# Queries of two attention layers: projected per pair of head groups, unpadded, and spread by transfers

## The chip, the cores and the metric

The kernel runs on one core of one Trainium2 chip. The core has five engines that work side by side: TensorE (matmuls, in the profile PE, its weight loads PEld), VectorE (DVE), ScalarE (ACT), GpSimd (POOL) and SyncE (SP, which issues transfers). Each engine has a queue of its own and takes its instructions in order. The metric is the device time of one execution in microseconds; the whole program, four layers, is one launch.

## What is computed

The reference is a stack of four layers, each a cross attention followed by a feed-forward part with experts. The change touches the cross attentions of layers 2 and 3. Their core, cut to what matters:

```python
# layer 2: B=2 batches, T=512 queries, T_ctx=1024 keys, 16 heads of 16
q = (x @ Wq + bq).reshape(B, T, H, D).transpose(0, 2, 1, 3)
kv = context @ Wkv + bkv
k, v = jnp.split(kv, 2, axis=-1)
att = jnp.einsum('bhtd,bhsd->bhts', q, k) * (1.0 / jnp.sqrt(D))
att = jnp.where(causal[None, None], att, -jnp.inf)
att = jax.nn.softmax(att, axis=-1)
y = jnp.einsum('bhts,bhsd->bhtd', att, v)
return y.transpose(0, 2, 1, 3).reshape(B, T, C) @ Wp + bp

# layer 3: no causal mask, no bias, and rotary embedding of queries and keys
def _apply_rope(t):
    cos, sin = _rope_tables(t.shape[2], t.shape[3], t.dtype)
    return t * cos[None, None] + _rotate_half(t) * sin[None, None]
q = _apply_rope((x @ Wq).reshape(B, Nq, H, hd).transpose(0, 2, 1, 3))
k = _apply_rope(k)
attn = jax.nn.softmax(jnp.einsum('bhqd,bhkd->bhqk', q, k) * scale, axis=-1)
```

Here `x` is the layer-normed state, 2 x 512 rows of 256 numbers. All is done in 32-bit floats.

## The kernel before, in words

`attend16` is the attention of layers 2 and 3. A head has only 16 dimensions, while the matmul array has 128 rows. So four heads make a group, and each head gets 32 rows of the array: 16 for its dimensions, one for its key maximum (row 16) and the rest zero. There are 2 batches x 4 groups = 8 groups, numbered 0 to 7; groups 0 to 3 are batch 0. The tile `qT` holds the queries of one group in this padded form, 128 rows by 512 queries; `kT` holds its keys the same way.

The padding is made by the weights: `Wq_pad` (`_pad_cols`, L2095) has zero columns where a head's 16 rows end, so one projection of a group gives `qT` padded. That is `prep(n)` (L1541): two matmul calls over the two halves of the 256 input channels (`mm2`, L187 to L190), 128 output rows by 512 queries. A float32 matmul call shows in the trace as two matmul records. In layer 2 the bias is added by VectorE as the sum is read (L1548). In layer 3, except for group 0, ScalarE copies the sum (L1559), one more matmul with a permutation matrix turns it (L1562, tile `rot`), VectorE multiplies that by the sines (L1564, `rs`), and GpSimd multiplies the copy by the cosines and adds (L1565, L1566).

The work of a group is cut into slots, 8 in layer 2 and 16 in layer 3. In slot h of group n, TensorE computes two score blocks of a first pass over group n (L1624, queries against keys), of which VectorE takes the maxima (L1628 with the mask in layer 2, L1633 in layer 3), and two score blocks of a second pass over an earlier group (L1683), whose exponentials ScalarE writes as `p` (L1684). The second pass runs LAG = slots + 2 behind the first. `with_maxima` (L1640) lies between them: it turns the negated maxima into row 16 and adds them to `qT`, which gives `qA`, the queries of the second pass. `product` (L1649) multiplies `p` with the values, and after the last one ScalarE copies the sum (`ou`, L1664). Its reciprocals take a way through memory: `Inverse` (L216) packs the rows by four transfers (L225), VectorE inverts them (L228, kept in program order on its engine), and five more transfers (L230, L233) spread them over a tile with the tag `rec`, of which there are two buffers. `divide` (L1693) multiplies on GpSimd.

All score, projection and rotation results go to banks of PSUM taken from one ring of seven (`bank`, L1529). A bank is taken again when its reader is done.

The order on TensorE is the program's order (`pe_in_order`, L1751). Extra work is cut into pieces that are called between slots (`Pieces`, L262): `prep` of the next group is put in front of the list at h = 0 of each group (L1756), and one piece is called in a slot, in odd slots of layer 3 and even ones of layer 2 (not in slot 0). Keys of the next group are fetched at h = 2 by SP (`fetch16`, L1476: four transfers of 16 rows for `kT`, L1480, and in layer 3 eight more for the turned keys, L214) and rotated at h = 8 (`rotate`, L200, on VectorE and GpSimd). The expert weights of layer 2's feed-forward part (L661, four transfers of 2 MB) are held back until group 0's maxima are in, and then run during the first groups. The parameters of an attention (`params16`, L1432) are loaded by SP during the feed-forward part before it.

Before the change no transfer of `attend16` is issued by ScalarE; elsewhere in the kernel ScalarE issues stores of keys and values (L806, L825).

Of the kernel before, what the change touches and what calls it, by code (L numbers as in the profile page):

```python
# [10 lines left out]
F32 = mybir.dt.float32  # L11
I32 = mybir.dt.int32
AF = mybir.ActivationFunctionType
# [4 lines left out]
P = 128  # L18
D = 256
B = 2  # L20
N = 512
S = 1024
# [11 lines left out]
def tile_kernel(ctx: ExitStack, tc: tile.TileContext, d: dict, out: bass.AP):  # L34
    nc = tc.nc
# [164 lines left out]
    def rotate(k, turned, cos, sin, pin=keep):  # L200


        for hf in range(2):
            hs = slice(hf * 512, (hf + 1) * 512)
            pin(nc.vector.tensor_mul(turned[:, hs], turned[:, hs], sin[:, hs]))  # L205
            pin(nc.gpsimd.tensor_mul(k[:, hs], k[:, hs], cos[:, hs]))  # L206
            nc.gpsimd.tensor_add(k[:, hs], k[:, hs], turned[:, hs])  # L207
# [947 lines left out]
    pre = ExitStack()  # L1155
# [276 lines left out]
    def params16(L, rotary, bias):  # L1432

        pre = ExitStack()
        cp = pre.enter_context(tc.tile_pool(name=f"{L}p", bufs=1, reuse_waits="tile"))
        bq = bvp = perm16 = wqr = cos = sin = None
        loads = []

        def ld(pool, shape, src, name):
            t = pool.tile(shape, F32, tag=name, name=name)  # L1440
            loads.append((t, src))
            return t

        def ld_rows(pool, src, name):
            rows, cols = src.shape
            return ld(pool, [P, rows // P, cols], src.rearrange("(t p) f -> p t f", p=P), name)

        def ld_bc(pool, src, name):
            return ld(pool, [P, src.shape[0]], src.partition_broadcast(P), name)

        one17 = ld(cp, [P, 1], d["c_one17"], "one17")
        if bias:
            bq, bvp = ld(cp, [P, 4], d[f"{L}_bq_pad"], "bq"), ld(cp, [P, 4], d[f"{L}_bv_pad"], "bvp")
        if rotary:
            cos, sin = ld(cp, [P, S], d["c_cos16"], "cos"), ld(cp, [P, S], d["c_sin16"], "sin")
            perm16 = ld(cp, [P, P], d["c_perm16"], "perm16")
            wqr = ld_rows(cp, d[f"{L}_Wq_turned"], "wqr")
        wq = ld_rows(cp, d[f"{L}_Wq_pad"], "wq")
        wo = ld_rows(cp, d[f"{L}_Wo_pad"], "wo")
        bo = ld_bc(cp, d[f"{L}_bo"], "bo")  # L1460
        sel16 = ld(cp, [P, P], d["c_sel16"], "sel16")
        cmask = None
        if not rotary:
            cmask = cp.tile([P, 4, P], F32, tag="cmask", name="cmask")
            nc.gpsimd.memset(cmask[:, 0:3, :], 0.0)
            make_causal_mask(nc, cmask[:, 3, :], NEG)
            cmask = cmask.rearrange("p t f -> p (t f)")

        return pre, cp, loads, (perm16, one17, wqr, bvp, bq, cos, sin, wq, wo, bo, sel16, cmask)

    def key_rows(k, one17, engine):

# [29 lines left out]
    def attend16(L, params, nkt, causal, rotary, front, norm, V, keys):  # L1502
# [11 lines left out]
        with (  # L1514
# [2 lines left out]
            tc.tile_pool(name=f"{L}t", bufs=2, reuse_waits="tile") as tmp,  # L1517
            psum(1, f"{L}ps") as ps,
        ):
            perm16, one17, wqr, bvp, bq, cos, sin, wq, wo, bo, sel16, cmask = params  # L1520
            kTs, turns, nms, fetched_keys = keys
            if nms is None:
                nms = maxima16(cp)
# [8 lines left out]
            groups = [(b, g) for b in range(B) for g in range(4)]  # L1532
            G = [dict() for _ in groups]
            oTs, ready = {}, []

            def fetch(n):
                G[n].update(kT=kTs[n % 3], v=V[groups[n][0]])
                if n >= fetched_keys:
                    fetch16(L, n, kTs[n % 3], turns[n % 2] if rotary else None, keep if n > 1 else as_is)

            def prep(n):  # L1541

                b, g = groups[n]
                qT = G[n]["qT"] = kp.tile([P, N], F32, tag="qT", name="qT")
                pq = bank("pq")
                mm2(pq, wq, slice(g * P, (g + 1) * P), xT, slice(b * N, (b + 1) * N))
                if not rotary:
                    nc.vector.tensor_scalar(qT, pq, bq[:, g : g + 1], None, ALU.add)  # L1548
                    yield
                    return  # L1550
                if n == 0:
                    rot = bank("rot")
                    mm2(rot, wqr, slice(0, P), xT, slice(0, N))
                    nc.vector.tensor_mul(qT, pq, cos[:, 0:N])
                    rs = tmp.tile([P, N], F32, tag="rs", name="rs")
                    nc.vector.tensor_mul(rs, rot, sin[:, 0:N])
                    nc.vector.tensor_add(qT, qT, rs)
                    return
                nc.scalar.copy(qT, pq)  # L1559
                yield  # L1560
                rot = bank("rot")
                nc.tensor.matmul(rot, perm16, qT, start=True, stop=True)  # L1562
                rs = tmp.tile([P, N], F32, tag="rs", name="rs")
                nc.vector.tensor_mul(rs, rot, sin[:, 0:N])  # L1564
                nc.gpsimd.tensor_mul(qT, qT, cos[:, 0:N])  # L1565
                nc.gpsimd.tensor_add(qT, qT, rs)  # L1566
                yield
# [171 lines left out]

            fetch(0)  # L1740
            fetch(1)
            norm_to(xn, X, norm)
            for _ in into_xT(0):
                pass
# [6 lines left out]
            with pe_in_order():  # L1751
                while t <= NG * slots + LAG + 6 or pieces.queue:
                    n, h = divmod(t, slots)
                    steps = range(t, t + (2 if n >= NG or n == 0 else 1))
                    if h == 0 and n + 1 < NG:
                        pieces.add(prep(n + 1), 2 if rotary else 1, True)  # L1756
                    if h == 2 and 0 < n < NG - 1:
                        fetch(n + 1)
                    if t == 2:
# [3 lines left out]
                        pieces.add(second_batch(), 7)  # L1763
                    if rotary and h == 8 and 0 < n < NG - 1:
                        rotate(G[n + 1]["kT"], turns[(n + 1) % 2], cos, sin)
                    for first in ((False, True) if h % 2 == 0 else (True, False)):
                        if first and n < NG:
                            first_pass(n, h)
                        elif not first:
                            for u in steps:  # L1770
                                m, k = divmod(u - LAG, slots)
                                if 0 <= m < NG:
                                    second_pass(m, k)
# [317 lines left out]
def _per_partition(v):  # L2091
    return v.reshape(2, P).T


def _pad_cols(w):  # L2095

    p = np.zeros((w.shape[0], 16, 32), w.dtype)
    p[:, :, :16] = w.reshape(-1, 16, 16)
    return p.reshape(w.shape[0], 512)


def _arrays(i):
# [20 lines left out]
        "L3_onw_p": _per_partition(i["L3_ffn_out_norm_w"]),  # L2123
        "L2_bo": i["L2_xattn_bp"],
        "L3_bo": i["L3_xattn_bo"],
        "L2_bq_pad": _pad_cols(i["L2_xattn_bq"][None]).reshape(4, P).T,
        "L2_bk": _per_partition(i["L2_xattn_bkv"][:D]),
        "L2_bv_pad": _pad_cols(i["L2_xattn_bkv"][None, D:]).reshape(4, P).T,
        "c_sign": np.tile(np.repeat(np.float32([-1.0, 1.0]), 32), 2)[:, None],
# [18 lines left out]
    a["c_cos64"], a["c_sin64"] = _rotary_table(S, 64, 64)  # L2148
    a["c_cos16"], a["c_sin16"] = _rotary_table(S, 16, 32)

    a["c_cos16"].reshape(4, 32, S)[:, 16] = 1.0
    for n in (
        "L0_xattn_Wq", "L0_xattn_Wkv", "L0_xattn_Wo", "L0_xattn_bo",
# [4 lines left out]
    ):  # L2158
        a[n] = i[n]
    for L, wo in (("L2", "L2_xattn_Wp"), ("L3", "L3_xattn_Wo")):  # L2160
        a[f"{L}_Wq_pad"] = _pad_cols(i[f"{L}_xattn_Wq"])
        turn = np.arange(P) ^ 8
        a[f"{L}_Wq_turned"] = a[f"{L}_Wq_pad"][:, 0:P][:, turn]
        a[f"{L}_Wk"] = i[f"{L}_xattn_Wkv"][:, :D]
        a[f"{L}_Wv"] = i[f"{L}_xattn_Wkv"][:, D:]
        a[f"{L}_Wo_pad"] = _pad_cols(i[wo].T).T
# [20 lines left out]
```

## Time and profile before

| what | before |
|---|---|
| runs | 2099.61, 2102.62, 2104.06 us; median 2102.62 |
| the profiled execution | 2102.66 us, span 2100.6 us |
| mean granted TensorE clock | 0.965 |
| layer 2's attention | first projection of queries read at 1200.3 us, last `qA` of it written at 1311.1 us |
| layer 3's attention | first projection of queries read at 1530.1 us, last `qA` written at 1793.8 us |
| TensorE in 1600 to 1630 us | busy 30.00 of 30 us, clock 1.00 |
| ScalarE in 1600 to 1630 us | busy 17.34 of 30 us |
| TensorE in 1250 to 1270 us | busy 19.15 of 20 us, clock 1.00 |
| ScalarE in 1250 to 1270 us | busy 9.01 of 20 us |
| matmuls `pq` (all layers) | 160 records, median 592 ns |
| matmuls `rot` of L1562 | 14 records, median 645 ns |

How to read the lines that follow further down: a line of the timeline gives the start in microseconds from the start of the span, the time taken, engine and line, operation, output <- inputs with their shapes, and how many instructions are merged in it. In brackets stands the idle time of the engine just before it and what ended that. Engines with a q at the end are queues: the time there is that of issuing a transfer, not of moving its data. Matmuls are pipelined and their ends are modelled, so the step from one start to the next is a safer price than the length of a record.

### The profile page before, as it was taken

Reading aid. Unit: us, or ns where it says so; the run is one execution under the profiler, and the core shown is the slowest. Engines: PE = TensorE matmul, PEld = TensorE weight load, DVE = VectorE, ACT = ScalarE, POOL = GpSimd, SP = SyncE. Lnnn points to the kernel's source line nnn. Section 1 sums busy time; section 2 is a strip of 40 time slices with the busy share of each in tenths; the row PEclk is TensorE's granted clock in tenths of the full one; section 3 lists DMA queues with packets and bytes.
Section 4 is the critical chain, followed back from the end, with each engine's and each line's share of the span. In section 5 each row is a group of like instructions: output and inputs, shape, how many; then the busy total and the mean of one; then the engine's idle time right before and its main releaser. Section 6 shows DMA issues by size and latency. Waiting matters only on the chain. (4 is left out here: it accounts for less than half of the span.)

```text
span 2100.6 us, 29379 instructions
## 1 busy us (share of the span) xinstructions
PE 1974.4 (94%) x11246; PEld 1153.0 (55%) x11246; DVE 1033.8 (49%) x2016; ACT 865.4 (41%) x1692; POOL 504.0 (24%) x496
## 2 busy tenths in 40 slices
PE   7999999999898999999899899899989999879996
PEld 3444444434565455555558644589833333478994
DVE  7666766672112566666531366410167767332223
ACT  4444444433112666656411344412225545624333
POOL 2223223311111212211213223453242321112220
PEclk9999999999999999999989999899979999979998
DMA  4111111137883311100326241478400100278882
GB/s 141 46 31 43 29 34 28 31 125 270 352 350 137 86 31 44 48 21 1 123 92 236 104 179 26 136 266 322 166 10 16 32 17 21 78 294 368 351 319 93
DMA packets 84742, 267.62 MB, mean 127 GB/s; under 512 B 22768, under 2 KB 54896, under 8 KB 75888
## 3 DMA queue, kind: packets, MB, share of 16 engines
q1 hardware_dynamic: 67600, 147.50, 20.9%
q0 software_dynamic: 10656, 106.57, 13.3%
q10 hardware_dynamic: 6336, 11.54, 1.4%
q8 instruction: 95, 1.56, 0.3%
q14 instruction: 55, 0.45, 0.1%
HBM read 232.70 MB, written 24.82 MB: 123 GB/s over the span
## 5 line engine op out<-in xcount | busy, mean ns | idle before, releaser
L1684 ACT ACTIVATE p<-s 128x512 f32<-128x512 f32 (+3 forms) x384 | 186.9, 546 | 153.7 <-PE s L1683 101.9
L1624 PE MATMUL s<-kT,qT 32*128 32x512 f32 (+3 forms) x768 | 201.6, 602 | 6.0 <-DVE mx L1633 1.9
L190 PE MATMUL pa<-sT,w 128*128 128x128 f32 x1536 | 188.6, 278 | 9.5 <-DMA w<-in_L_experts_dram,wrow 9.0
L1683 PE MATMUL s<-qA,kT 32*128 32x512 f32 (+3 forms) x768 | 195.2, 593 | 0.8 <-DVE qA L1646 0.6
L190 PEld LDWEIGHTS pa<-sT,w 128*128 128x128 f32 x1536 | 184.4, 195 | 14.2 <-issue 12.0
L1633 DVE TENSOR_REDUCE mx<-s 128x1 f32<-128x512 f32 x256 | 165.4, 694 | 52.2 <-PE s L1624 33.4
L695 PE MATMUL y<-w,hT 128*128 128x256 f32 x768 | 175.9, 381 | 2.9 <-DVE hT L691 2.0
L1289 ACT ACTIVATE p<-s,nm 128x512 f32<-128x512 f32 x192 | 129.3, 686 | 80.6 <-DVE nm L1286 80.6
L1107 ACT ACTIVATE p<-s 128x1024 f32<-128x1024 f32 x128 | 124.1, 1021 | 89.8 <-PE s L1102 89.8
L1108 DVE TENSOR_SCALAR p<-p 128x1024 f32<-128x1024 f32 x128 | 108.8, 858 | 97.0 <-ACT p L1107 96.8
L1286 DVE TENSOR_REDUCE nm<-s 128x2 f32<-128x1024 f32 x96 | 113.2, 1221 | 83.7 <-PE s L1282 83.7
L207 POOL TENSOR_TENSOR kT<-kT,turned 128x512 f32<-128x512 f32 x62 | 99.6, 1613 | 228.4 <-DVE turned L205 199.8
L695 PEld LDWEIGHTS y<-w,hT 128*128 128x128 f32 x768 | 141.8, 190 | 22.1 <-DVE hT L691 3.2
L691 DVE TENSOR_TENSOR hT<-act,pg 128x512 f32<-128x512 f32 x58 | 39.9, 688 | 186.6 <-PE pg L190 165.1
L1113 DVE TENSOR_TENSOR acc<-acc,p 128x1024 f32<-128x1024 f32 x96 | 129.7, 1351 | 2.8
L1033 PE MATMUL o<-p,v 128*64 128x512 f32 x512 | 125.4, 606 | 2.9 <-DVE p L1108 2.8
L1102 PE MATMUL s<-qT,kT 64*128 64x512 f32 x512 | 127.2, 615 | 0.0
L583 POOL DMA_INDIRECT yd<-yo,slot_to x60 | 59.6, 993 | 271.2 <-ACT yo L742 128.8
L206 POOL TENSOR_TENSOR kT<-kT,cos 128x512 f32<-128x512 f32 x62 | 87.6, 1425 | 121.3 <-DMA turned<-kT 72.1
L1303 PEld LDWEIGHTS pt<-ident,p 128*128 128x128 f32 x768 | 84.5, 141 | 52.9 <-issue 19.8
L571 POOL DMA_INDIRECT xs<-xd,slot_of x60 | 57.8, 964 | 231.6 <-PE pt L577 134.4
L190 PE MATMUL pg<-sT,w 128*128 128x128 f32 x928 | 113.3, 275 | 0.0
(357 smaller groups left out, 3161.2 us busy)
## 6 DMA issues: line engine op xcount, KB each, us to landing
w<-in_L_experts_dram SPq DMA_DIRECT2D x8, 3200.0 KB
w<-in_L_experts_dram SPq DMA_DIRECT2D x8, 3072.0 KB
w<-in_L_experts_dram SPq DMA_DIRECT2D x8, 2048.0 KB
w<-in_L_experts_dram SPq DMA_DIRECT2D x8, 1536.0 KB
turned<-kT SPq DMA_DIRECT2D x60, 128.0 KB
kd<-sk ACTq DMA_DIRECT2D x28, 256.0 KB
yg<-yd SPq DMA_DIRECT2D x24, 256.0 KB
vd<-sv ACTq DMA_DIRECT2D x16, 256.0 KB
```

What stands on the lines that cost most here:

```text
L190: nc.tensor.matmul(ps_ap, lhsT[:, dc, lcols], rhs[:, dc, rcols], start=(dc == 0), stop=(dc == 1))
L695: x = nc.tensor.matmul(y, hT[:, f, :], w2[:, f, :], start=(f == 0), stop=(f == FT - 1)).ins
L1033: nc.tensor.matmul(G[n]["o"][64 * j : 64 * j + 64, :], V[g, b][:, kt, pr * P + 64 * j : pr * P + 64 * j + 64], p[:, j, :], start=(kt == 0) ...
L1102: nc.tensor.matmul(s1[:, j, :], G[n]["kT"][r, kt * P : (kt + 1) * P], G[n]["qT"][r, :], start=True, stop=True)
L1107: nc.scalar.activation(p, s1, AF.Exp, scale=0.125)
L1113: nc.vector.tensor_add(G[n]["acc"], G[n]["acc"], p)
L1286: nc.vector.tensor_reduce(nm[:, qt, :, c], s1, AX.X, ALU.max, negate=True)
L1289: nc.scalar.activation(p[:, j, :], s1[:, j, :], AF.Exp, bias=nm[:, qt, j, c : c + 1], accum_out=l[:, qt, j, c : c + 1],)
L1624: nc.tensor.matmul(s1[:, :w], qT[r, qt * P : (qt + 1) * P], kT[r, c * 512 : c * 512 + w], start=True, stop=True)
L1633: G[n]["max"] = nc.vector.tensor_reduce(mx[:, qt, j, c : c + 1], s1, AX.X, ALU.max).ins
L1683: nc.tensor.matmul(s2[:, qs], kT[r, kt * P : (kt + 1) * P], qA[r, qs], start=True, stop=True)
L1684: G[n]["exp"] = nc.scalar.activation(p[:, j, qs], s2[:, qs], AF.Exp, scale=0.25).ins
```

## The change

Groups 0 and 1 are prepared as before (which also leaves zeros in the unused rows of the two `qT` tiles). From group 2 on, one projection with the unpadded weights gives the queries of two groups at once: 8 heads x 16 = 128 rows. Layer 2 adds the bias on ScalarE, layer 3 copies, turns and rotates the pair once, with tables of 16-row pitch. The pair lies in a tile of the tag `rec`. Then each of the two groups gets its queries by four transfers on ScalarE's queue, each of 16 rows of 512 numbers, into rows 0, 32, 64 and 96 of a fixed `qT` tile. In layer 2 the transfers are issued in the `prep` piece, in layer 3 at slot 6 of the group before.

```diff
         if bias:
-            bq, bvp = ld(cp, [P, 4], d[f"{L}_bq_pad"], "bq"), ld(cp, [P, 4], d[f"{L}_bv_pad"], "bvp")
+            bq, bvp = ld(cp, [P, 2], d[f"{L}_bq_pad"], "bq"), ld(cp, [P, 4], d[f"{L}_bv_pad"], "bvp")
...
         wq = ld_rows(cp, d[f"{L}_Wq_pad"], "wq")
+        wqs = ld_rows(cp, d[f"{L}_Wq"], "wqs")
+        bqs = ld(cp, [P, 2], d[f"{L}_bq"], "bqs") if bias else None
...
+            qTs = [kp.tile([P, N], F32, tag=f"qT{i}", name=f"qT{i}", bufs=1) for i in range(2)]
+            pair = {}
+
+            def queries(n):
+
+                b, g = groups[n]
+                pq = bank("pq")
+                mm2(pq, wqs, slice(g // 2 * P, (g // 2 + 1) * P), xT, slice(b * N, (b + 1) * N))
+                q = pair[0] = tmp.tile([P, N], F32, tag="rec", name="pair")
+                if not rotary:
+                    nc.scalar.activation(q, pq, AF.Identity, bias=bqs[:, g // 2 : g // 2 + 1])
+                    return
+                nc.scalar.copy(q, pq)
+                yield
+                cos_q, sin_q, perm = tables
+                rot = bank("rot")
+                nc.tensor.matmul(rot, perm, q, start=True, stop=True)
+                rs = tmp.tile([P, N], F32, tag="rs", name="rs")
+                nc.vector.tensor_mul(rs, rot, sin_q)
+                nc.gpsimd.tensor_mul(q, q, cos_q)
+                nc.gpsimd.tensor_add(q, q, rs)
+                yield
+
+            def spread_queries(n):
+
+                qT, r = qTs[n % 2], n % 2 * 64
+                for j in range(4):
+                    nc.scalar.dma_start(qT[32 * j : 32 * j + 16, :], pair[0][r + 16 * j : r + 16 * j + 16, :])
...
             def prep(n):
 
                 b, g = groups[n]
-                qT = G[n]["qT"] = kp.tile([P, N], F32, tag="qT", name="qT")
+                qT = G[n]["qT"] = qTs[n % 2]
+                if n > 1:
+                    if g % 2 == 0:
+                        yield from queries(n)
+                    if not rotary:
+                        spread_queries(n)
+                        yield
+                    return
...
             fetch(0)
             fetch(1)
+            if rotary:
+                tables = [
+                    load(kp, [P, n], d[f"c_{k}16s"], f"{k}_q", 1) for k, n in (("cos", N), ("sin", N), ("perm", P))
+                ]
...
                     if h == 0 and n + 1 < NG:
-                        pieces.add(prep(n + 1), 2 if rotary else 1, True)
+                        pieces.add(prep(n + 1), (n == 0 or n % 2) * 2 if rotary else 1, True)
...
                         rotate(G[n + 1]["kT"], turns[(n + 1) % 2], cos, sin)
+                    if rotary and h == 6 and 0 < n < NG - 1:
+                        spread_queries(n + 1)
...
-        a[f"{L}_Wq_pad"] = _pad_cols(i[f"{L}_xattn_Wq"])
+        a[f"{L}_Wq"] = i[f"{L}_xattn_Wq"]
+        a[f"{L}_Wq_pad"] = _pad_cols(i[f"{L}_xattn_Wq"])[:, 0 : 2 * P]
```

The padded weights and bias are cut to groups 0 and 1, and the tables `c_cos16s`, `c_sin16s` and `c_perm16s` (16-row pitch, 512 columns for the first two) are added to the inputs.

## The prediction

> **What bounds the kernel now.** I read the page's first part, then the timeline of one steady group of each of the two attentions, then the rows of the transfers on the queues. The page says that TensorE is busy for nearly the whole span:
>
> ```profile
> PE   1974.4 (94%) x11246; PEld 1153.0 (55%) x11246; DVE 1033.8 (49%) x2016; ACT 865.4 (41%) x1692; POOL 504.0 (24%) x496
> ```
>
> An average doesn't say what a removed matmul is worth, so the stage has to be looked at. In layer 3 (timeline, the group that prepares the queries of group 3):
>
> ```profile
> 1598.94 1.98 PE L190 MATMUL pq<-xT,wq 128*128 128x512 f32 x4
> 1600.86 0.70 PE L1683 MATMUL s<-qA,kT 32*128 32x512 f32 x2
> ...
> 1604.35 1.12 PE L1562 MATMUL rot<-qT,perm 128*128 128x512 f32 x2
> ...
> 1605.40 0.70 PE L1683 MATMUL s<-qA,kT 32*128 32x512 f32 x2
> ...
> 1608.29 1.09 ACT L1684 ACTIVATE p<-s 128x512 f32<-128x512 f32 x2 [0.58 <-PE s L1683]
> ...
> 1610.05 1.08 ACT L1684 ACTIVATE p<-s 128x512 f32<-128x512 f32 x2 [0.68 <-PE s L1624]
> ```
>
> TensorE goes from the projection to the next score at once, so a projection takes 1600.86 - 1598.94 = 1.92 us of its line and a rotation 1605.40 - 1604.35 = 1.05. ScalarE idles 0.58 to 0.68 between its pairs of exponentials. That is no free room: the scores rotate through 7 banks, each slot takes 4, and in every second slot the last score matmul takes the bank that the first exponential of the slot before gives back. What ScalarE loses there, TensorE loses.
>
> Layer 2 (the same group there) is tighter:
>
> ```profile
> 1227.52 1.98 PE L190 MATMUL pq<-xT,wq 128*128 128x512 f32 x4
> ...
> 1227.68 1.09 ACT L1684 ACTIVATE p<-s 128x512 f32<-128x512 f32 x2 [1.17 <-PE s L1683]
> ...
> 1230.60 1.09 ACT L1684 ACTIVATE p<-s 128x512 f32<-128x512 f32 x2 [1.84 <-PE s L1683]
> ...
> 1232.04 1.29 ACT L1684 ACTIVATE p<-s 128x384 f32<-128x384 f32 x3
> ...
> 1232.61 0.29 PEld L1683 LDWEIGHTS s<-qA,kT 32*128 32x128 f32 x2 [0.58 <-ACT p L1684]
> ```
>
> From 1230.60 on ScalarE has no gap, and TensorE's load at 1232.61 waits for its exponential: for these two slots ScalarE sets the pace, and a delay of the exponentials at 1230.60 goes through to the group's end.
>
> What a transfer costs its queue:
>
> ```profile
> 1226.06 1.71 SPq L1480 DMA_DIRECT2D kT<-kd  x4
> ...
> 1232.19 3.53 SPq L225 DMA_DIRECT2D inv<-ou  x4
> ...
> 1190.13 0.36 ACTq L806 DMA_DIRECT2D kd<-sk  x1
> 1190.54 1.07 ACT L863 COPY V<-pk 128x512 f32<-128x512 f32 x2 [3.04 <-DMA yg<-yd]
> ```
>
> Four transfers of 16 rows of 2 KB, the new ones' very shape, hold their queue for 1.71. The last two rows are ScalarE's own: a store waited for another transfer to land (the profile names yg), and the copy behind it waited with it, idle for 3.04.
>
> **The change part by part.** Call groups 2, 4 and 6 first of a pair (projected, for layer 3 rotated, and spread) and 3, 5, 7 second (spread alone). D is the time for which four transfers hold ScalarE; I take 1.71.
>
> TensorE, removed. The second groups lose a projection in both layers and a rotation in layer 3: there 3 x (1.92 + 1.05) = 8.91 us, TensorE setting the pace. In layer 2, without the 1.92 of projection, the exponentials of 1230.60 could start when the pair before them ends, at 1227.68 + 1.09 = 1228.77: at most 1.83 a group.
>
> Layer 2, second groups. The transfers stand behind the pair of exponentials of 1227.68 and wait for no work of ScalarE's own, so they can issue while the second of the pair runs, from about 1228.22, to 1228.22 + D = 1229.93. The exponentials then start 0.67 earlier than before, so 3 x 0.67 = 2.0 is won of 3 x 1.83.
>
> Layer 2, first groups. The bias moves from VectorE (0.75, L1548) to ScalarE; the nearest row is L805, an activation with bias of the same shape, 0.69. In terms of the rows above it starts when the projection is read, at 1229.54, and ends 1230.23; the transfers read what it writes and wait for it, to about 1230.25 + D = 1231.96. The exponentials behind them are 1.36 late, and TensorE's scores with them: 3 x 1.36 = 4.1 lost. VectorE's six saved 0.75 buy nothing: it sat idle 0.96 for the projection.
>
> Layer 3, all six. The transfers stand at slot 6, behind the exponentials of slot 5; GpSimd's sum is done by then (its last operation on the queries, from 1606.90, takes 1.26, to 1608.16). In first groups they go from 1608.83, the second exponential's start, to 1610.54, 0.49 past the old start of 1610.05. In second groups, where the gap between pairs is 0.47 (row of 1592.47), they end 0.69 late. Cost 3 x 0.49 + 3 x 0.69 = 3.5.
>
> The sum is 12 D - 23.8: each of 12 spreads costs D less the room it finds. With D = 1.71 it is -3.3 us.
>
> Ends for D: 1.2, if each takes 0.30, the shortest of L1480 (sum -9.4), and 2.41, the usual four of inv<-ou (L225: +5.1; 3.53 in the loaded stretch). If transfers can't issue while an exponential runs, nine spreads lose another 0.54 each, +4.9. I take the row of the same shape.
>
> The loaded stretch. The windows from 1213 to 1229 show DMA shares of 0.96 to 1.04 (layer 2's expert weights, issued at 1210.93), and the first spread falls into it at about 1216.4. The trace's landing events put the kT<-kd transfers issued from 1226.06 in it at 9 us, those from 1241.22, outside it, at 2.0. The queries are first read at 1223.8 (two heads) and 1225.5 (the others), some 1.4 later now. Price 0 to 4 us, once; I take 0.5, since they have a ring of their own. Also, the trace's transfers of SP and ScalarE take eight landing semaphores in turn and each waits for the one eight before it. With four more in the turn, group 3's keys fall behind the four weight loads, the last landing at 1235.2, and the next four of L225 go out near 1237.5 instead of 1235.2; VectorE's reciprocal stood at 1237.00. Price 0 to 2.7, I take 0.6. Elsewhere the eighth transfer before is an old one, or rec<-inv, landed as the spread issues.
>
> At nothing: three copies less on ScalarE in layer 3 (0.585 each, behind idle time of 1.33), three rs products on VectorE, six operations of 1.27 on GpSimd (idle 19.70 before them). The smaller wq and the new wqs move equal bytes. The added loads (wqs, bqs, three tables) are issued by SP in its idle time: between its rows of 1513.26 and 1538.26 for the tables; without that cover five issues of 0.45, 2 us. The pair shares the two rec buffers with the reciprocals' rows; an old row has been divided slots earlier, or the other buffer is free, so none waits.
>
> Total: -3.3 + 0.5 + 0.6 = -2.2. The profiled execution took 2102.66 (span 2100.6), the median of the runs is 2102.62, so the base is the same: **2100.4**.
>
> [...] The row of 1.71 for four says that the issuer is held for the issue alone.
>
> **The rivals.** *One: ScalarE hardly feels the transfers.* For it: 41% busy and an issue of 0.33 alone on its queue (L806). Against it: the back-to-back row of SP. At D = 1.2 -9.4, with the first-use prices 2094.4; with no hold at all and no loss from the moved bias -14.4, 2088.3. Take 2093. From D under 1.54 the sum is beyond -4.2.
>
> *Two, the other side: ScalarE's exponentials queue behind transfers that wait.* One mechanism: the in-order queue of ScalarE, just behind slot 2 in layer 2 and slot 5 in layer 3, held by issues that start only when the running exponential is done. Price 9 x 0.54 = 4.9 on top of the sum: 2105.4; with D = 2.41 too, +5.1 + 4.9 + 1.1 = +11.1, 2113.8. It decides from D of 2.24 on, or from an added wait of 0.5 at each spread. For it: the 3.04 of 1190.54. Against it: at 491.68 a store is issued on ScalarE's queue while a copy from 491.62 runs.
>
> *Three: the queries arrive late,* the loaded stretch alone at its bounds: -3.3 + 4 + 2.7 = +3.4, 2106.1. Elsewhere five slots or more lie between issue and first read, against 2 us of landing. Also the change might not do what it says, the projections gone but the time spent as TensorE's waits: that is the forecast driven to zero.
>
> **How the numbers follow.** Forecast 0.45, rival one 0.27, two 0.20, three 0.08. A measurement here tells some 0.2%, 4.2 us, from no change. Of the forecast 0.13 lies beyond -4.2 and 0.01 beyond +4.2; rival one is all faster; two gives 0.18 slower, three 0.03. Faster 0.40, same 0.38, slower 0.22. The likeliest case's own range is 2096 to 2105; for 8 in 10 it reaches into rivals one and two, 2091 to 2109.
>
> **What would show it.** 12 matmul records of the projection less in layer 2, 12 and 6 of the rotation in layer 3; 48 transfers on ScalarE's queue. Right: four of them in about 1.7 us, starting before the exponential ahead has ended, and the next pair late by 0.5 to 0.7 in layer 3 and 1.4 after the moved bias. Layer 3 should be some 5.4 us shorter, layer 2 some 3 longer. Wrong: ScalarE waiting for a landing ahead of them, or TensorE waiting for a transfer at the first read of a group's queries; or no idle time of TensorE at all, which would be rival one.

## The result, and the profile after

The change made the kernel slower: 2113.70 us median of 4 runs (2113.05 to 2120.49) against 2103.34 (2099.61 to 2104.51), ratio 1.006, 95% interval 1.0035 to 1.0084. The forecast was 2100.4 with a range from 2091 to 2109, so the time lies outside it. The profiled execution of the changed kernel took 2113.05 us, its span is 2111.3.

The work that was to go is gone. First part of the page of the changed kernel:

```profile
PE 1977.1 (94%) x11216; PEld 1156.6 (55%) x11216; DVE 1024.6 (49%) x2007; ACT 865.9 (41%) x1692; POOL 497.9 (24%) x490
```

There are 30 matmul records less (11246 before), the 12 + 12 + 6 that were forecast, yet TensorE is busy 2.7 us longer. The mark that shows where is the write of `qA` between a group's two passes, once a group (L1646 before, L1683 after). The steps from one to the next, in us, from the timelines; interval k contains the preparation of group k + 1, so 1, 3 and 5 hold a first of a pair, 2, 4 and 6 a second:

| kernel | layer 2, intervals 1 to 7 | sum | layer 3, intervals 1 to 7 | sum |
|---|---|---|---|---|
| before | 15.4 13.7 13.6 13.6 13.6 16.3 14.7 | 100.9 | 34.6 31.6 31.6 31.6 41.0 32.2 28.3 | 230.9 |
| after | 17.1 16.4 18.6 13.2 17.4 15.1 14.7 | 112.7 | 35.2 29.8 33.4 29.8 42.9 29.8 28.2 | 229.1 |

Layer 3 gained 1.8 us where 5.4 was forecast, layer 2 lost 11.8 where about 3 was; layer 2 starts 3.4 later, the stretch between the two attentions is 4.5 shorter and the tail 1.7 longer. (Runs below whose code is the same up to there write the first `qA` anywhere from 1204.4 to 1217.4, so those three and interval 1 are not read as the change's. The rows are of one execution each: e2 and e12 below, whose layer 2 code is that of after, took 112.8 and 111.7 in layer 2, but e12 spread them otherwise, 14.5, 17.2, 15.7 and 16.2 in intervals 2 to 5.) Four places carry the loss.

**Layer 3, a first group.** Timeline of the changed kernel, 1648 to 1653:

```profile
1647.84 0.60 ACT L1721 ACTIVATE p<-s 128x512 f32<-128x512 f32 x1 [1.32 <-PE s L1661]
...
1648.12 1.26 POOL L1557 TENSOR_TENSOR pair<-pair,rs 128x512 f32<-128x512 f32 x1
...
1649.42 0.52 ACTq L1564 DMA_DIRECT2D qT<-pair  x1
...
1649.98 0.60 ACT L1721 ACTIVATE p<-s 128x512 f32<-128x512 f32 x1 [1.54 <-PE s L1720]
1650.01 1.86 ACTq L1564 DMA_DIRECT2D qT<-pair  x3
...
1650.63 0.70 PE L1720 MATMUL s<-qA,kT 32*128 32x512 f32 x2 [0.45 <-ACT p L1721]
...
1651.91 1.57 ACT L1721 ACTIVATE p<-s 128x512 f32<-128x512 f32 x3 [1.33 <-DMA qT<-pair]
1652.56 0.62 PE L1695 MATMUL o<-p,V 128*32 128x256 f32 x2 [0.79 <-ACT p L1721]
```

The first transfer does not stand behind the pair of exponentials but between its two halves, and it waits there for GpSimd's sum, which ends at 1648.12 + 1.26 = 1649.38. The second exponential, free to run at 1648.44, starts at 1649.98. Its idle time is put down to a score matmul, but that was done by 1647.74 (1647.15 and 0.59): what held it is the queue entry ahead of it. TensorE then waits 0.45 and 0.79. A transfer takes 0.60 here, four of them with the first's 0.5 some 2.4.

**Layer 3, a second group.** The transfers wait here too, for something else. The same view, 1607 to 1613:

```profile
1608.86 0.69 DVE L1683 TENSOR_TENSOR qA<-nmT,qT 128x512 f32<-128x512 f32 x1
...
1609.58 1.80 ACTq L1564 DMA_DIRECT2D qT<-pair  x3
...
1611.42 0.60 ACT L1721 ACTIVATE p<-s 128x512 f32<-128x512 f32 x1 [2.97 <-DVE mx L1670]
...
1612.07 1.12 PE L1695 MATMUL o<-p,V 128*32 128x256 f32 x8 [0.37 <-ACT p L1721]
```

The write of `qA` is the last read of the `qT` tile that the transfers fill. It ends at 1609.55 and the first transfer goes out at 1609.58; in the two other second groups it is 0.03 us as well. In the source this write stands at slot 0 and the transfers at slot 6, so the built order has moved them ahead by some five slots. ScalarE stands 2.97 in all and TensorE 0.37, and the group takes 29.8 where 28.9 is possible (e4 below).

**Layer 2, a first group.** The same view at the third interval:

```profile
1252.35 0.69 ACT L1547 ACTIVATE pair<-pq,bqs 128x512 f32<-128x512 f32 x1 [0.77 <-PE pq L190]
...
1253.07 2.44 ACTq L1564 DMA_DIRECT2D qT<-pair  x4
...
1255.56 1.08 ACT L1721 ACTIVATE p<-s 128x512 f32<-128x512 f32 x2 [2.51 <-DMA qT<-pair]
1256.20 1.30 PE L1661 MATMUL s<-kT,qT 32*128 32x384 f32 x2 [0.98 <-ACT p L1721]
```

ScalarE stands 2.51 and TensorE 0.98. The wait itself is short. What follows it is not, as the windows of the same stretch show (columns: stretch, its length, busy time of PE, PEld, DVE, ACT and POOL with counts, the granted clock, the DMA share and GB/s):

```profile
1253.20:1256.60 3.40, 2.42 (x21) 1.13 (x20) 2.30 (x10) 1.04 (x3) 0.00 (x0) 1.00 0.16 39
1256.60:1260.00 3.40, 3.40 (x14) 0.70 (x12) 0.62 (x2) 2.17 (x6) 1.22 (x3) 0.50 0.02 2
1260.00:1263.40 3.40, 3.40 (x24) 1.90 (x24) 1.14 (x3) 0.88 (x3) 0.41 (x1) 0.50 0.01 1
```

TensorE was busy 2.42 of 3.40 us, and for the next 6.8 us its granted clock is 0.50, though it is busy all through. There are three such stretches in layer 2's groups, from 1242.9, 1256.6 and 1287.3, besides one of 3.4 us from 1215.6. The profile of before has none between its first and last `qA` except one of 3.4 us from 1211.1.

**Layer 2, the second interval.** Timeline of the changed kernel, 1231 to 1246:

```profile
1231.25 9.22 SPq L1482 DMA_DIRECT2D kT<-kd  x4
...
1240.63 2.46 SPq L225 DMA_DIRECT2D inv<-ou  x4
...
1244.36 0.25 DVE L228 RECIPROCAL inv<-inv 128x16 f32<-128x16 f32 x1 [3.47 <-DMA inv<-ou]
...
1245.32 0.79 PE L1661 MATMUL s<-kT,qT 32*128 32x128 f32 x2 [3.88 <-DVE nm L1665]
```

SyncE's fourth key transfer went out at 1240.17 only: it takes the landing semaphore of the last expert weight load (103 in the trace, issued at 1215.74), which landed at 1240.15. The third takes that of the load before it and went out at 1234.01, 0.02 after that had landed too. The packing of the reciprocals stands behind it, VectorE's reciprocal is pinned in its order and waits 3.47, the maxima behind that are late, TensorE idles 3.88, and the clock is 0.50 from 1242.9 on.

### The profile page after: what moved, and what is told of

Its sections match the earlier page's. It is cut to its first block, busy times and chain, and to the rows that moved or that the text cites. A ratio compares the mean times of both kernels' runs of the same rounds, so it can differ in the third digit from the quotient of the medians.

```text
span 2111.3 us, 29375 instructions
## 1 busy us (share of the span) xinstructions
PE 1977.1 (94%) x11216; PEld 1156.6 (55%) x11216; DVE 1024.6 (49%) x2007; ACT 865.9 (41%) x1692; POOL 497.9 (24%) x490
## 3 DMA queue, kind: packets, MB, share of 16 engines
q0 software_dynamic: 10656, 106.57, 13.2%
q10 hardware_dynamic: 7872, 13.11, 1.7%
## 5 line engine op out<-in xcount | busy, mean ns | idle before, releaser
L1661 PE MATMUL s<-kT,qT 32*128 32x512 f32 (+3 forms) x768 | 208.8, 611 | 10.9 <-DVE nm L1665 4.3
L190 PEld LDWEIGHTS pa<-sT,w 128*128 128x128 f32 x1536 | 184.8, 195 | 14.6 <-issue 12.3
L207 POOL TENSOR_TENSOR kT<-kT,turned 128x512 f32<-128x512 f32 x62 | 100.9, 1634 | 244.5 <-DVE turned L205 199.0
L1695 PE MATMUL o<-p,V 128*32 128x256 f32 (+3 forms) x1200 | 111.1, 429 | 6.8 <-ACT p L1721 3.4
```

The lines of the kernel that those rows point to most:

```text
L190: nc.tensor.matmul(ps_ap, lhsT[:, dc, lcols], rhs[:, dc, rcols], start=(dc == 0), stop=(dc == 1))
L1661: nc.tensor.matmul(s1[:, :w], qT[r, qt * P : (qt + 1) * P], kT[r, c * 512 : c * 512 + w], start=True, stop=True)
```

## The experiments

Times are medians, ratios against runs of the kernel before on the same chip.

**e1, e2: one layer alone.** In e1 layer 2 prepares as before (`n >= (2 if rotary else 99)`, its padded weights whole, no `wqs`), in e2 layer 3 does.

> The change in layer 3 alone; layer 2's attention as before the change. Theory A (the four issues of a spread hold ScalarE for 2.44 us where 1.71 was assumed, and layer 2 loses more by stalls of TensorE that halve its clock): the prediction's sum for layer 3 with D = 2.44 is -8.91 + 3 x 1.22 + 3 x 1.42 = -1.0 us, the trace of after shows -1.8 between its qA; so 2101 to 2103 us. Theory B (the loss is the landing of the queries and the turn of the landing semaphores, the same in every group of both layers): a loss here too, 2106 to 2109. If ScalarE hardly felt the transfers: 2094 to 2096.

> The change in layer 2 alone; layer 3's attention as before. Theory A: all of the loss is here. Issue alone by the prediction's sum with D = 2.44: -2.0 + 4.1 + 6 x 0.73 = +6.5 us, 2110; with the stalls and half-clock stretches seen in the trace of after +11 to +13, 2114 to 2117. Theory B: about half of the loss, 2107 to 2109. A half-clock stretch should stand again near the second and third group; if there is none and the time is still above 2113, the clock is not part of it.

e1 2105.97 (1.0021, 1.0002 to 1.0041), e2 2115.70 (1.0058, 1.0038 to 1.0077). Layer 2's intervals in e2 are those of after within 0.2, half-clock stretches included: the loss is layer 2's. Layer 3 is no gain in this form: 231.9 in e1, with the 29.8 and 33.4 of after and longer groups at the start and the change of batch. e1 came out above its 2101 to 2103.

**e3: the transfers on SyncE's queue.**

```diff
-nc.scalar.dma_start(qT[32 * j : 32 * j + 16, :], pair[0][...])
+nc.sync.dma_start(qT[32 * j : 32 * j + 16, :], pair[0][...])
```

> As after, but the 48 transfers are issued on SyncE's queue in place of ScalarE's. Theory A: ScalarE's hold is gone in all 12 spreads (12 x 2.44 less the room that they found), while the late keys and the late reciprocal of layer 2's second and third group stay: 2092 to 2100 us, and the exponentials no longer wait for the issue of qT<-pair. Theory B: nothing changes but the issuer, 2110 to 2116.

**e4: no transfers.**

```diff
 qT, r = qTs[n % 2], n % 2 * 64
-for j in range(4):
-    nc.scalar.dma_start(...)
+return
```

> As after without the 48 transfers: groups 2 to 7 reuse the queries left by groups 0 and 1 (the projection of a pair, its bias or rotation stay). What the removed matmuls are worth when nothing is paid for the spread. Theory A: the prediction's sum without hold and with no loss from the moved bias, -14.4 us, or -11.4 with a bias that still costs 3 x 1: 2089 to 2092, no half-clock stretch in layer 2's groups. If the removed matmuls only turned into TensorE's waits: 2100 or more, and the transfers would cost only what is above that.

e3 2104.51 (1.0012, 0.9993 to 1.0032), above what was expected. e4's queries are others, the experts get other rows, and 640 more matmul records run behind the attentions (2217 us), so only its intervals are read:

| kernel | layer 2 | sum | layer 3 | sum |
|---|---|---|---|---|
| e3 SyncE | 17.0 18.6 14.9 12.3 13.6 15.2 14.7 | 106.2 | 34.6 28.9 31.6 28.9 42.4 28.8 28.2 | 223.4 |
| e4 none | 16.6 12.4 13.6 12.3 13.6 15.2 14.7 | 98.4 | 34.6 28.9 31.6 28.9 42.4 28.8 28.2 | 223.4 |

This is the ceiling: 2.5 us in layer 2 and 7.5 in layer 3. Layer 3's second groups win 8.8; interval 5, with the change of batch, gives 1.4 back here (42.4) and next to nothing in e9, e10, e13 and e14 (41.1). In layer 3 the transfers on SyncE's queue are free. A first group takes the time it took before (31.6, 13.6), so the bias on ScalarE costs nothing by itself. In e3 the second interval is worse than in after: the spread and the keys now wait in one queue behind the weights.

**e5, e6: layer 2 pairs only from group 4 on** (`n >= (2 if rotary else 4)`, all four columns of padded weights kept beside `wqs`), the transfers on ScalarE's queue in e5 and on SyncE's in e6.

> Layer 2 uses pairs only from group 4 on (groups 2 and 3 project their own padded queries as before), so that no spread is issued while the expert weights load; layer 3 as after. Theory A, the turn of the landing semaphores: the keys of group 3 no longer wait for the last weight load, the reciprocal of group 1 comes in time, and the intervals between the qA of layer 2 that took 16.4 (second) and 18.6 us (third) with the change become 13.7 and about 16, layer 2 in all (first to last qA) 105 to 108 instead of 112.7: 2107 to 2110 us. Theory C: the half-clock stretches come from the issues that hold ScalarE, wherever they stand: the later groups keep theirs and the gain is under 2.5 us, 2111 or more.

> As the run before, with the transfers on SyncE's queue. If the two losses are the issue on ScalarE and the turn of the landing semaphores, and nothing else, both are gone: layer 2 from first to last qA 99 to 100 us (98.4 without any transfer, plus 1.2 for a projection that group 3 has again), layer 3 223.4; against the kernel before -1.3 and -7.5: 2094 to 2098 us, faster than both. If SyncE's own transfers are pushed back by the 48: 2100 or more.

e5 2124.39 (1.0101, 1.0075 to 1.0127), e6 2113.51 (1.0043, 1.0025 to 1.0062): both missed, though layer 2 came out as expected or shorter (103.2 and 100.1; layer 3 231.5 and 221.7). The waits of TensorE behind layer 2's attention in e6 say why (columns: who, for whom, us, times, longest):

```profile
PE pa L190 <- DMA w<-in_L_experts_dram: 13.0, 1, 13.0
```

No load of expert weights goes out during their attention (the first at 1379.39 in e5 and 1374.18 in e6, 1214.35 in after); that the two weight tiles held side by side left no memory for them is likely, but not shown. So these two don't test the turn of the semaphores by itself. One number of e5 stays: its third interval, a first group with its spread on ScalarE and no half-clock stretch, takes 15.0, 1.4 more than 13.6.

**e7: DRAM as the source; e8: half of the transfers on ScalarE.**

```diff
-nc.scalar.dma_start(qT[32 * j : 32 * j + 16, :], pair[0][...])
+nc.scalar.dma_start(qT[32 * j : 32 * j + 16, :], kd[16 * j : 16 * j + 16, 0:N])    # e7
+(nc.scalar if j % 2 else nc.sync).dma_start(qT[...], pair[0][...])                 # e8
```

> As after, but each transfer of a spread reads 16 rows of the keys in DRAM, of the same size, into the same rows of qT, instead of the pair in SBUF: the queries of groups 2 to 7 are keys, so the experts get other rows and only the time up to the last qA is read. The prediction took 1.71 us for four from such a row. If the source is what sets the issue time: 0.42 to 0.43 each, four in 1.7, and layer 3 by the prediction's sum (each spread costs what exceeds the room of 1.02 to 1.22) 223.4 + 3 x 0.49 + 3 x 0.69 = 226.9 at most, against 229.1. If ScalarE's queue is slower than SyncE's whatever the source: 0.5 to 0.6 each, and 229.

> As after, but of the four transfers of a spread two are issued on ScalarE's queue and two on SyncE's. D on ScalarE is about 1.2. If a spread costs only what exceeds the room ScalarE has (0.47 to 0.68 between pairs plus the running exponential), layer 3 is within 1 us of the 223.4 without any hold, 223.4 to 224.5. If each microsecond of issue costs the same, half of the 5.7 stays: 226.3. Layer 2 keeps the stall of its second and third group, 105 to 109 from first to last qA.

Timeline of e7, ScalarE's queue at the start of a group of layer 3:

```profile
1637.91 1.25 ACTq L1565 DMA_DIRECT2D qT<-kd  x3
...
1639.27 0.37 ACTq L1565 DMA_DIRECT2D qT<-kd  x1
```

1.25 + 0.37 = 1.62 for four, where the same tile from SBUF takes 2.44: the source sets the issue time, not the queue. (The queries are keys here, so the total of 2226.88 is not read.) But layer 3 takes 223.4, not 226.9: its third interval is 31.6, with nothing lost, second groups take 29.2, 0.3 to 0.4 lost. Keys need not wait for GpSimd, and the hold is shorter too, so this run doesn't part the two. e8 (2110.80, 1.0031, 1.0011 to 1.0051) gives 226.4, the sum that a price per microsecond of issue would give; its intervals fit that price less well. Second groups lose 0.2 to 0.3 at half the hold (0.9 at the whole), the first groups of intervals 3 and 5 still 0.8, and there the transfer again goes out when GpSimd's sum is done, 0.98 after the exponential ahead has ended. That was a hint that the place counts besides the hold.

**e9, e13: the change in layer 3 alone, its transfers elsewhere.** e9 is e1 with SyncE's queue; e13 is e1 with ScalarE's, kept in program order at slot 10. **e12** is after with that second edit:

```diff
-                    if rotary and h == 6 and 0 < n < NG - 1:
+                    if rotary and h == 10 and 0 < n < NG - 1:
...
-nc.scalar.dma_start(qT[...], pair[0][...])
+(keep if rotary else as_is)(nc.scalar.dma_start(qT[...], pair[0][...]))
```

> The change in layer 3 alone with its 24 transfers on SyncE's queue; layer 2's attention, its weights and their memory as before the change. Theory A: layer 3 from first to last qA 222 to 224 us against 230.9 before, nothing else moved, no 13 us wait for expert weights as in the run with pairs from group 4 on: 2094 to 2098 us, faster than both kernels. If the layer 3 gain is given back behind the attention: 2101 or more.

> As after, but layer 3's transfers are kept in program order at slot 10, behind a whole pair of exponentials, so they no longer wait for GpSimd's sum as in after (there the first starts at 1649.42, 0.98 us after the exponential ahead has ended). What the hold alone costs: by the prediction's sum with D = 2.44, 31.6 + 1.2 = 32.8 us for a first group (33.4 in after) and 28.9 + 1.4 = 30.3 for a second (29.8 in after), layer 3 231 us; total 2112 to 2117. If the wait for GpSimd made the whole loss of the first groups, they take 31.6 to 32.0.

> The change in layer 3 alone, on ScalarE's queue, with its transfers kept in program order at slot 10; layer 2 as before. If the place is all that was wrong in layer 3: 222 to 225 us from first to last qA as with SyncE's queue (222.1), total 2094 to 2100 us. If SyncE's queue was what helped: 229 to 232 in layer 3 and 2101 to 2106.

e9 2095.88 (0.9962, 0.9945 to 0.9978), e12 2106.81 (1.0016, 0.9998 to 1.0034), e13 2094.85 (0.9953, 0.9931 to 0.9975). Layer 3 takes 222.1, 223.1 and 222.1. In e12 and e13 ScalarE issues the same four transfers for the same time, and the third interval takes 31.6, second groups 28.8 to 28.9 (one of e12's, whose last transfer took 1.96 to issue, 29.7): what no transfers at all take. Both sums for e12, 32.8 and 30.3, were wrong. Timeline of e12:

```profile
1661.51 0.59 ACT L1721 ACTIVATE p<-s 128x512 f32<-128x512 f32 x1
1661.67 1.88 ACTq L1564 DMA_DIRECT2D qT<-pair  x3
...
1662.86 0.64 PE L1695 MATMUL o<-p,V 128*32 128x256 f32 x8
...
1663.43 0.70 PE L1661 MATMUL s<-kT,qT 32*128 32x512 f32 x2
...
1663.60 1.67 ACT L1721 ACTIVATE p<-s 128x512 f32<-128x512 f32 x3 [1.50 <-DMA qT<-pair]
```

The issues begin under the running pair here (the first at 1661.12) and wait for nothing. ScalarE stands 1.50 where 0.47 to 0.88 is usual between pairs, and TensorE goes on without a gap: exponentials up to a microsecond late cost nothing here. In after the second exponential was 1.54 late on its own, and the next pair behind the other three transfers as well.

**e10, e11: GpSimd's queue,** for all 48 transfers (e10), for layer 2's groups 2 and 3 alone (e11).

```diff
-nc.scalar.dma_start(...)
+nc.gpsimd.dma_start(...)                                                      # e10
+(nc.gpsimd if n < 4 and not rotary else nc.scalar).dma_start(...)             # e11
```

> As after, with all 48 transfers on GpSimd's queue. If GpSimd's transfers have landing semaphores of their own, neither ScalarE nor the turn of SyncE's and ScalarE's transfers feels them: layer 2 98 to 101 us from first to last qA without a stall of the second and third group, layer 3 223 to 224, 2092 to 2098 us. If the loss lies in the transfers themselves (landing in the loaded stretch), layer 2 stays at 105 or more. If GpSimd's issue holds its own mask and rotation work, layer 2 loses 1 us or more in each group.

> As after, with the two spreads of layer 2's groups 2 and 3 (8 transfers) on GpSimd's queue and the 40 others on ScalarE's. The price of the turn alone. Theory A: the second interval between qA of layer 2 falls from 16.4 to 12.4 to 13.7 us, the reciprocal no longer waits 3.47, and without that stall the third (still with a spread on ScalarE) falls from 18.6 to 15 to 17; layer 2 105 to 108 us against 112.7, layer 3 as after (229): 2105 to 2109 us. If the stall is not from the turn: 2112 or more.

e10 2097.23 (0.9977, 0.9963 to 0.9990), e11 2109.43 (1.0040, 1.0022 to 1.0058). The trace's landing events put GpSimd's transfers on semaphores of their own (111 to 118 in before and after, where SyncE and ScalarE share 100, 102, 103 and 105 to 109), SyncE's four keys go out in 1.7 us (9.22 in after) and VectorE doesn't wait for inv<-ou. Yet the second intervals are 20.6 and 19.1. Windows of e10:

```profile
1225.20:1228.60 3.40, 2.35 (x21) 1.23 (x14) 3.02 (x11) 0.73 (x4) 0.81 (x2) 1.00 1.01 361
1228.60:1232.00 3.40, 2.68 (x20) 1.38 (x24) 0.72 (x4) 0.45 (x2) 1.23 (x3) 0.50 0.99 419
```

The clock halves here too, for 17.1 us in both profiles, the weights still loading at its start (DMA share 0.99). Ahead of it in e10's trace stands a wait for queries that land late:

```profile
1228.46 0.66 PE L1661 MATMUL s<-kT,qT 32*128 32x128 f32 x2 [0.72 <-issue]
```

The last two of group 2's four transfers, issued by 1220.5, land at 1228.37 and 1229.76, and TensorE's first scores that read them start at 1228.46 and 1229.85, 0.09 later each. In e11 the second lands at 1226.77, and TensorE, idle for 1.44, goes on at 1226.86, 0.09 later again; the profile puts this wait down to VectorE, which was done at 1226.43. So in these two profiles the turn was mended and the time lost again, to the landing and the clock. Both executions are slower than their kernel's median (2102.86 and 2118.28), so not every run need have lost as much.

**e14, e15, e16: layer 2 once more.** e14: layer 2's spread leaves `prep` and is kept in program order at slot 5, between the exponentials of 384 columns; layer 3 as in e12. e15: the four weight loads wait for the last group's `qA` (`return ready[0] if rotary else ready[7]`). e16:

```diff
-nc.scalar.activation(q, pq, AF.Identity, bias=bqs[:, g // 2 : g // 2 + 1])
+nc.vector.tensor_scalar(q, pq, bqs[:, g // 2 : g // 2 + 1], None, ALU.add)
```

> The change in both layers on ScalarE's queue; layer 3's transfers at slot 10, layer 2's kept in program order at slot 5, between its exponentials of 384 columns, instead of right behind the bias. Theory place: a first group takes 13.6 to 14.5 us instead of 15.0 (17.4 and 18.6 with a halved clock), with no half-clock stretch after the third interval; layer 2 102 to 107 us, total 2098 to 2106. Theory hold: ScalarE sets the pace of layer 2 in these slots, 2.44 us cost the same there, 15 to 17 us for a first and 13.3 to 15 for a second group, layer 2 110 to 114, total 2107 to 2114.

> As after, but the four loads of expert weights that run during layer 2's attention are held until the last group's qA, so nothing of the attention stands beside them or behind them in the turn; the feed-forward part then waits for them, and only layer 2's intervals are read. If the late reciprocal comes from the loads: the second interval 12.4 to 13.7 us instead of 16.4, no wait of VectorE for inv<-ou of 3 us, and the third 15 to 16 instead of 18.6. If the spreads alone make it: 16 and 18 again.

> As after, but layer 2's bias of a pair is added by VectorE, as before the change, instead of ScalarE. The prediction charged first groups of layer 2 1.36 us for bias and hold together, 0.69 of it the bias (2.09 with D = 2.44). If the bias counts: first groups some 0.7 us shorter where the clock is full (15.0 to 14.3), and TensorE's share in their window stays above the 0.72 below which the clock halves: layer 2 104 to 109 us, total 2105 to 2110. If the hold alone counts: no change, 2112 to 2115.

| kernel | time, ratio | layer 2 | sum |
|---|---|---|---|
| e14 | 2102.34, 0.9987 (0.9970 to 1.0004) | 20.6 18.9 13.6 12.3 13.6 17.4 13.6 | 110.0 |
| e15 | 2122.65, 1.0088 (1.0061 to 1.0114) | 18.2 12.3 14.9 15.7 14.9 15.1 14.7 | 105.8 |
| e16 | 2113.29, 1.0035 (1.0008 to 1.0063) | 17.8 14.7 17.6 13.2 15.0 15.3 14.7 | 108.2 |

e15 settles the second interval: without the loads it takes 12.3, as with no transfers, and the keys and reciprocals of that place go out in

```profile
1233.32 2.79 SPq L1482 DMA_DIRECT2D kT<-kd  x4
1239.88 2.46 SPq L225 DMA_DIRECT2D inv<-ou  x4
```

Its first groups, at full clock, take 14.9. e16 changes nothing that the runs can tell; its fifth interval at full clock is 15.0 without the bias on ScalarE, as with it. But it leaves the bias in the way, as its timeline shows:

```profile
1271.69 0.75 DVE L1547 TENSOR_SCALAR pair<-pq,bqs 128x512 f32<-128x512 f32 x1 [0.96 <-PE pq L190]
...
1272.47 2.44 ACTq L1564 DMA_DIRECT2D qT<-pair  x4
...
1274.96 0.60 ACT L1721 ACTIVATE p<-s 128x512 f32<-128x512 f32 x1 [4.05 <-DMA qT<-pair]
```

The transfers stand in ScalarE's queue until VectorE's bias is done, and ScalarE idles 4.05, where in after 0.77, the bias of 0.69 and 2.51 took about as long. So the run doesn't part the bias from the hold. e14's third to fifth intervals are those of no transfers (13.6, 12.3, 13.6) with the bias on ScalarE and four issues of 2.4: place again, not hold. But there the queries of group 2 are issued later, into the weight loads. Timeline of e14:

```profile
1217.30 0.60 ACTq L1564 DMA_DIRECT2D qT<-pair  x1
...
1217.94 1.88 ACTq L1564 DMA_DIRECT2D qT<-pair  x3
...
1224.71 0.76 PE L1660 MATMUL s<-kT,qT 32*128 32x128 f32 x2 [1.75 <-issue]
1226.31 0.76 PE L1660 MATMUL s<-kT,qT 32*128 32x128 f32 x2 [0.83 <-DMA qT<-pair]
```

The trace's landing events of these four end at 1224.6, 1226.2, 1227.7 and 1228.4, some 7 to 9 us after the issue; TensorE waits for them twice, and the clock is 0.50 for the 20.5 us from 1224.3. No run kept layer 2's gain and the loads in the attention together; its 1.2 us longer end (31.0 for the last two intervals against 29.8) was not looked into.

## Why the prediction was wrong, step by step

Most of the miss of 13.3 us is layer 2's, 11.8 lost where 3.2 was put: what failed there is the price of the loaded stretch, 1.1, and the clock, which the sum left out. Layer 3 adds 3.6; what failed there is the place of the transfers and the price of a late exponential.

**The removed matmuls** were priced about right: 2.7 a second group in layer 3 (31.6 to 28.9) where 2.97 was put; 7.5 in all for 8.91 (8.8 without interval 5). In layer 2 1.1 to 1.3 a group was to be had, 0.67 was put and the fourth and sixth interval won 0.4 and 1.1. There too the transfers did not issue while the second exponential ran: in all three second groups they go out with `qA` written, 0.03 to 0.04 after it (1231.49, 1266.54, 1297.22).

**D.** 1.71 was taken from `kT<-kd` as "the new ones' very shape", and 2.41 of `inv<-ou` kept as the far end. It was 2.44. The two rows differ in where they read from, and e7 shows that this is what decides (1.62 from DRAM, 2.44 from SBUF, on one queue). The shape of the destination was the wrong likeness.

**The step that failed in layer 3** is not D, though. It is two sentences: "What ScalarE loses there, TensorE loses", on which 12 D - 23.8 rests, and "The transfers stand at slot 6, behind the exponentials of slot 5; GpSimd's sum is done by then". The first is refuted by e12 and e13, where the whole 2.44 is issued and nothing is lost. The second took the place from the source, but the instructions of ScalarE are ordered anew when the kernel is built: the trace has the transfers of a first group inside a pair, waiting for GpSimd, and those of a second some five slots earlier, waiting for `qA`. With the place mended layer 3 gains 7.8 us against before in e12, 2.4 more than the forecast had it win. In after it fell 3.6 short of its forecast: first groups lost 0.7, 1.8 and 1.9 against before where 0.49 each was put, and second ones won 6.1 in all where 8.91 - 3 x 0.69 = 6.8 was.

**Layer 2's first groups** were to lose 1.36. At full clock they lost 1.3 to 1.4 (e5 15.0, e15 14.9, against 13.6), so the size held, by luck: with D = 2.44 the same sum gives 2.09. ScalarE was that late, its exponentials starting 3.21 after the projection was read (1255.56 against 1252.35), where 1.06 was usual (1230.60 against 1229.54); but not all of these 2.15 reached the group. Bias and hold are not parted by any run. What was not in the sum at all is the clock. The third interval took 18.6 and the fifth 17.4: 3.6 and 2.4 beyond 15.0 go with the half-clock stretches, 9.4 us at 0.50 in the third and 6.8 in the fifth.

**The loaded stretch.** The mechanism was named, four more in the turn of eight semaphores, priced 0 to 2.7 and taken as 0.6. It cost 16.4 - 12.3 = 4.1 (e15), its clock stretch included, and 2.2 to 2.4 in e12 and e16 (14.5 and 14.7), whose transfers and loads there are the same: SyncE's queue stood 9.22 behind the last load, and with it not only the keys but everything that follows. That it was the turn is read from the trace of after; e15 takes away the loads as well. The bound left out what a stalled VectorE holds up behind its pinned reciprocal. The late landing (0 to 4) did not show as a wait in after; it did in e10, e11 and e14. The queue of their own is in the pages (q10, 11.54 MB before and 13.11 after), but in after group 2's queries landed 6.2 to 8.3 us after their issue on it in the loaded stretch, the four issued from 1253.07, outside it, after 1.9 to 2.0.

**At nothing** were the tables' issues, the moved rs products and the pair's use of the rec buffers. No run separates them; e9 and e13 carry layer 3's share of them and still win 7 to 10 us.

**The rivals.** Rival two's 2113.8 is the measured time, and its condition, an added wait of 0.5 at a spread or D from 2.24, was met. Its mechanism holds only in part: a wait there is, but for GpSimd's sum in layer 3's first groups and for `qA` in second ones, and transfers do issue under a running exponential (1650.01 above, the exponential of 1649.98 running). The sum agrees by chance, since it prices nine such waits and no clock. Rival one, that ScalarE hardly feels the transfers, is what e13 shows for layer 3, in another place in the queue. Of the signs named, the record counts came true; layer 3's 5.4, layer 2's 3 and the 1.7 us did not.

## What to carry to other kernels

A transfer in an engine's queue costs what it makes the next instruction wait, so look up in the built order what stands behind it and what its source still waits for; pinned behind work that is already fed, four issues of some 2.4 us were free in layer 3, and where they waited for their source or their target they cost up to 1.9. Count added transfers in the turn of landing semaphores behind a large load: SyncE and ScalarE share eight here, and the key transfer on the last load's went out 6.2 us after the one ahead of it in the queue (1240.17 against 1234.01). Where matmuls stall, price the clock that may follow, not the stall alone: behind the 0.98 of the third interval it was 0.50 for 6.8 us.

Of what was run, the change in layer 3 alone with its transfers on ScalarE's queue at slot 10 (e13) or on SyncE's (e9) is faster than both kernels, 0.9953 and 0.9962 of before; the change in both layers with its transfers on GpSimd's queue (e10) comes next with 0.9977.

## What the runs showed of the hardware

**The clock.** In the clock records the half-clock stretches of layer 2's attention are whole multiples of 3.41 us: 3.4 and 6.8 in after, 17.1 in e10 and e11, 20.5 in e14. In windows of 3.41 us on the grid of these stretches, from 1225 to 1310, TensorE's records in after cover 0.564 of the full-clock window from 1239.5 and 0.713 (0.98 us short) of those from 1253.2 and 1283.9, and half clock follows each. The other full-clock windows there are covered 0.877 or more, and full clock follows all of them. In before all windows of that stretch are covered 0.890 or more, at 1.00. The 0.72 named for e16 lies between these figures; over both whole traces it is no sure sign: of the full-clock windows covered less, 30 are followed by half clock and 32 are not, of those covered more, 8 of 1080 are. In after the clock stayed at 0.50 for a second window though TensorE was busy 3.40 of 3.40 us in the first (from 1256.6); why it stayed low for 17 to 20 us in e10, e11 and e14 is open.

**Issuing.** On ScalarE's queue a transfer of 16 rows of 2 KB that waits for nothing takes 0.51 to 0.61 from SBUF (after; 2.4 for four) and 0.31 to 0.44 from DRAM (1.6 for four, e7). On GpSimd's it takes 0.48 to 0.60 from SBUF (e10), with landing semaphores apart from the eight that SyncE and ScalarE share. Three transfers whose semaphore was that of a weight load still under way went out 0.01 to 0.02 after it had landed (1235.22 in before, 1234.01 and 1240.17 in after).
